# A two-layer graph kernel: waits between engines, the place of TensorE's sums in a sorting stage, and blocks of 2, 4, 4, 6, 6, 6, 4 tiles

## The chip, the core and the metric

The kernel runs on one core of a Trainium2 chip. Its engines work side by side, each through its own queue in order: TensorE (PE, with weight loads shown apart as PEld), VectorE (DVE), ScalarE (ACT), GpSimd (POOL) and SyncE (SP). POOL also issues the indirect DMAs, which fetch or store one row per partition at addresses that are themselves data. The metric is the device time of one execution in microseconds, the median of several.

## The reference, cut to what matters

Two graph layers over 4,096 nodes with 128 features; `adj` has about 64 neighbours for a node.

```
# layer 0: attention with 8 heads
Wh  = einsum('nd,hde->hne', nodes, W)
e   = leaky_relu(f1[:, :, None] + f2[:, None, :])       # f1, f2: Wh times a1, a2
att = softmax(where(adj > 0, e, -9e15))
h   = elu(einsum('hnm,hmd->hnd', att, Wh))
x   = elu(concat(h) @ W1 + b1)
x1  = layernorm(nodes + x, gamma, beta)
# layer 1: quartiles of the kept neighbours, feature by feature
rank = cumsum(mask, axis=1) - 1
skip = where(num_nbr > 5, ceil(num_nbr / 2), 1)
keep = mask & ~(mask & ((rank + 1) % skip == 0))
svals = sort(where(keep, x1, big), axis=1)
agg  = mean over q in (.25, .5, .75) of svals[max(ceil(q * n_keep) - 1, 0)]
agg  = 0.5 * agg + 0.5 * x1
out  = agg @ W.T + b + x1
```

## The kernel before

A tile is 128 nodes, one per partition; there are 32 tiles. The kernel has two stages, `gat` for layer 0 and `sparse` for layer 1. Both gather: a node's neighbours are rows in memory, and each indirect DMA of POOL fetches one neighbour for each of 128 nodes.

**Neighbours (`Front`, within `gat`).** `scan` loads quarters of rows of `adj` (SP, L378, 512 KB each, three buffers), turns them into bits on ACT (L380, L387) and packs them into words by matmuls (L389) in two banks of PSUM. `first` and `second` (L402 on) pull the neighbours' numbers out of the words on DVE, eight at a time with MAX8 and MATCH_REPLACE8 (L188, L190). This goes by blocks of tiles, `BLOCKS = (4, 4, 6, 6, 6, 6)`. When a block's tiles are through, `place` (L447) orders its nodes by their number of neighbours, so that tiles of like counts arise, and POOL scatters the block's lists to `rows_d` (L541, one DMA a tile). From there SP reads each block's lists back (`indices`: ids L903, single columns `others` L919, and info L932). `keep` works out which neighbours layer 1 keeps and writes them to `meta_d` through SP. At the end `order` ranks all nodes by the number they keep, and 32 scatters of POOL write the ranks to `order_d` (L680). `pieces` makes a list of all these steps; `advance(n)` takes the next n of them. The attention's loop calls `advance(2)` once for each half tile, so the search for neighbours of later blocks is laid between the attention of earlier ones. Every engine takes the instructions in the order in which they are written.

**Attention (`gat`).** The loop runs over 64 half tiles. `load` has POOL gather the half tile's neighbours (nb, L971) into a ring of 6 buffers of 18 rows, three half tiles ahead, and once per tile the nodes' own rows (me, L947). `probabilities` computes the softmax (DVE L1054 to L1088, ACT L1073), `rows_sum` spreads the probabilities (DVE L1103) and sums the neighbours by matmuls (PE L1111). After every four half tiles `combine` makes x1 of two tiles, spread over the following half tiles as stages, and two scatters (L1197) write it to `x1_d`. These scatters wait for each other, since all write to the same tensor. After the last gather is issued, the rest of the list is worked off and the 32 scatters to `order_d` are issued:

```
            if u + 3 < 2 * NT:
                held[u + 3] = load(u + 3)
            elif late:
                advance(len(todo))
                for piece in late:
                    piece()
```

**Sorting (`sparse`).** It loads `order` from `order_d`, then for each tile an index row (info, L1867), the nodes' own rows (xs) and 50 to 100 kept neighbours (rows, L1713), again one indirect DMA each. A sorting network runs over a tile's rows, 128 features at once. A step of it is a `compare`: ACT copies the lower rows out (L1751), DVE writes min (L1756) and max (L1757) back. A copy of up to `SMALL = 4` pairs goes to SBUF (low_s), a larger one to PSUM (low, two buffers of four banks with 16 pairs each, so all eight banks). Steps where only one side is needed do without ACT (L1759, L1761). The steps of one tile's last part and the next tile's first part are interleaved. Tile 0's first part is cut into steps of at most `PAIRS // 2` pairs, so that it can begin before all rows have landed.

After a tile is sorted, `quantile` marks the places of the quartiles, and `pick` appends three pieces of work to a list `waiting`: ACT scales the rows at those places (picked, L1810), PE sums them (L1815, L1818) into PSUM, ACT copies the sum to comT (L1823). After four tiles `finish` appends the linear layer on PE (L1835 to L1837), ACT's copy to o (L1841) and the scatters to the output (L1845). Each compare with a copy takes at most one piece from this list. A piece that needs PSUM is taken by a compare of 5 to 12 pairs, and uses the last 512 columns of that compare's own buffer, which the compare leaves free:

```
                if waiting and waiting[0][0] == "copy":
                    waiting.pop(0)[1]()
                elif waiting and SMALL < k <= PAIRS - FOUR:
                    waiting.pop(0)[1](t[:, (PAIRS - FOUR) * D :])
                nc.vector.tensor_tensor(lows, packed, highs, op=ALU.min)
                nc.vector.tensor_tensor(highs, packed, highs, op=ALU.max)
```

The matmuls come before min and max in program order, and since both read or write the same buffer, min waits for the matmuls. What is left in `waiting` after the last tile is done in one go.

Of the kernel before, what the change touches and what calls it, by code (L numbers as in the profile page):

```python
# [50 lines left out]
P = 128  # L51
N = 4096
# [40 lines left out]
MOST = 16  # L93
# [4 lines left out]
BLOCKS = (4, 4, 6, 6, 6, 6)  # L98
# [13 lines left out]
BOUNDS = {  # L112
    4: (
# [203 lines left out]

class Front:
# [88 lines left out]
    def second(self, t, m, k1, cand):  # L407

        nc, one = self.nc, self.one
        k1, cand = k1[:, :m], cand[:, :m]  # L410
        sp = self.spill[:, t : t + m, :]
        wf, base = decode(nc, one, k1, f"1_{m}")
        rest = one.tile([P, m, C1], F32, name=f"rest1_{m}")
        peel(nc, one, wf, base, cand[:, :, :C1], rest, f"1_{m}")
# [5 lines left out]
        k2 = one.tile([P, m, C2], F32, name=f"k2_{m}")  # L420
# [5 lines left out]
        wf, base = decode(nc, one, k2, f"2_{m}")  # L426
        rest = one.tile([P, m, C2], F32, name=f"rest2_{m}")
        peel(nc, one, wf, base, cand[:, :, C1 : C1 + C2], rest, f"2_{m}")
        nc.vector.tensor_scalar(base, base, 127.0 * NG1, None, op0=ALU.add)
        nc.vector.scalar_tensor_tensor(rest, rest, float(NG1), base, op0=ALU.mult, op1=ALU.add)  # L430
        k3 = one.tile([P, m, C3], F32, name=f"k3_{m}")
# [5 lines left out]
        wf, base = decode(nc, one, k3, f"3_{m}")  # L437
        for r in range(PEELS):
            nxt = one.tile([P, m, C3], F32, name=f"rest3_{m}", bufs=2)
            at = C1 + C2 + C3 * r  # L440
            peel(nc, one, wf, base, cand[:, :, at : at + C3], nxt, f"3_{m}")
            wf = nxt
        left = one.tile([P, m], F32, name=f"left_{m}")
# [353 lines left out]
def gat(tc, nc, c, x, adj, xf_d, meta_d, order_d, flag_d, w, a1, a2, w1, b1, gamma, beta, x1_d):  # L797
# [25 lines left out]
    with ExitStack() as ctx:  # L823
# [307 lines left out]
        def combine(t, zT):  # L1131
# [64 lines left out]
            for j in range(TWO):  # L1196
                nc.gpsimd.indirect_dma_start(  # L1197
# [4 lines left out]
                )  # L1202

        held = {u: load(u) for u in range(3)}
# [5 lines left out]
        for u in range(2 * NT):  # L1210
            t, half = divmod(u, 2)
            if u + 3 < 2 * NT:
                held[u + 3] = load(u + 3)
            elif late:

                advance(len(todo))
                for piece in late:
                    piece()
                late = []
# [3 lines left out]
            if u + 1 < 2 * NT:  # L1223
                with ExitStack() as order:
                    for ins in behind:
                        order.enter_context(tc.issue_after(ins))
                    e, behind = probabilities(u + 1, held[u + 1], f1s[(u + 1) // 2])
            with ExitStack() as order:
                for ins in behind:
                    order.enter_context(tc.issue_after(ins))  # L1230
# [7 lines left out]
            advance(2)  # L1238
        for stages in going:
            for _ in stages:  # L1240
                pass
        advance(len(todo))
# [415 lines left out]
def plan(t):  # L1658
# [8 lines left out]
    first = steps(layers[:-merge], lambda i: i, PAIRS if t else PAIRS // 2)  # L1667
# [7 lines left out]
def sparse(tc, nc, c, x1_d, meta_d, order_d, w, b, out):  # L1675


    with tc.tile_pool(name="sp1", bufs=1) as one, tc.tile_pool(
# [15 lines left out]
        it = one.tile([P, 2 * MIDDLE], I32, name="it_p")  # L1694
        nc.gpsimd.iota(it, pattern=[[1, 2 * MIDDLE]], base=0, channel_multiplier=0)
        iota_p = one.tile([P, 2 * MIDDLE], F32, name="iota_p")
        nc.vector.tensor_copy(iota_p, it)
        order = one.tile([P, NT], I32, name="order")
        for i in range(4):
            nc.sync.dma_start(  # L1700
                out=order[:, ts(i, NT // 4)],
                in_=order_d[ts(i, N // 4), :].rearrange("(t p) c -> p (t c)", p=P),
            )

# [7 lines left out]
        def gather(row, info, col):  # L1712
            nc.gpsimd.indirect_dma_start(  # L1713
# [24 lines left out]
        def compare(rows, step):  # L1738
# [4 lines left out]
            if low and high:  # L1743
# [7 lines left out]
                nc.scalar.copy(packed, lows)  # L1751
                if waiting and waiting[0][0] == "copy":
                    waiting.pop(0)[1]()
                elif waiting and SMALL < k <= PAIRS - FOUR:
                    waiting.pop(0)[1](t[:, (PAIRS - FOUR) * D :])
                nc.vector.tensor_tensor(lows, packed, highs, op=ALU.min)  # L1756
                nc.vector.tensor_tensor(highs, packed, highs, op=ALU.max)  # L1757
# [45 lines left out]
        def pick(found, x1, comT):  # L1803
# [3 lines left out]
            def scale():  # L1807
                made["v"] = tp.tile([P, MOST, D], F32, name="picked", bufs=1)
                for i, (v, weight) in enumerate(found):
                    nc.scalar.mul(made["v"][:, i, :], v, weight)  # L1810
# [496 lines left out]
```

## Time and profile before

| | |
|---|---|
| timed runs (3) | 8,432.01 us median, 8,431.48 to 8,434.64 |
| the profiled execution | 7,646.96 us, its span 7,645.2 us |
| first neighbour gather issued | 142.51 us |
| last neighbour gather ends | 3,106.6 us |
| first sorting gather | 3,170.57 us |
| last DVE step ends | 7,632.9 us |
| DVE busy, share of the span | 5,831.7 us, 76% |
| POOL busy, share of the span | 4,343.5 us, 57% |
| ACT busy, share of the span | 2,214.1 us, 29% |
| PE busy, share of the span | 1,122.8 us, 15% |

The profiled execution is 785 us shorter than the timed median. All lines of the profile, and all durations, belong to the profiled one. In the lines, an entry such as `rows<-low,rows` names output and inputs, `x1022` the number of instructions; in the timeline the first two numbers are the start and the duration in us, and the bracket gives the engine's idle time before the instruction and what released it.

### The profile page before, as it was taken

The page shows a single profiled execution, that of the slowest core. Times are in us where ns is not written, and L with a number is a line of the kernel's source. Part 1 is how long each engine was busy: PE and PEld are TensorE (multiplying, and loading weights), DVE is VectorE, ACT ScalarE, POOL GpSimd, SP SyncE. Part 2 cuts the span into 40 slices and gives each one's busy share as a digit, 9 for nine tenths or more (in the row PEclk, how much of TensorE's full clock was granted, in tenths as well). Part 3 has the DMA queues.
Part 4 walks back from the last instruction along what each step waited for, and adds up shares of the span by engine and source line. Part 5 has one row for each costly group of instructions (what it writes and reads, how often), then busy time and mean ns, then how long its engine had stood idle before and what let it go on. Part 6 is the DMA issues. An engine that isn't in the chain of part 4 may idle for free. (4 is left out here: it accounts for less than half of the span.)

```text
span 7645.2 us, 31290 instructions
## 1 busy us (share of the span) xinstructions
PE 1122.8 (15%) x6047; PEld 946.8 (12%) x6047; DVE 5831.7 (76%) x9380; ACT 2214.1 (29%) x2301; POOL 4343.5 (57%) x4524
## 2 busy tenths in 40 slices
PE   3243333322222322100000000000000000000001
PEld 1232222222222222100000000000000000000000
DVE  8465555565223222399999999999999999999999
ACT  6020212100000000144344343434334433443433
POOL 2777677777777777565554645455536434554500
PEclk5566666666566666655555555555555555555555
DMA  6242324222222222111111111111101101111100
GB/s 205 57 121 56 107 62 121 60 55 56 47 56 56 56 56 56 40 44 34 40 35 30 41 31 37 30 36 34 38 23 41 34 24 33 36 35 29 33 1 1
DMA packets 219057, 380.95 MB, mean 50 GB/s; under 512 B 129283, under 2 KB 129412, under 8 KB 218852
## 3 DMA queue, kind: packets, MB, share of 16 engines
q0 software_dynamic: 145808, 308.58, 15.3%
q1 hardware_dynamic: 72898, 70.23, 3.1%
q14 instruction: 156, 1.28, 0.1%
q8 instruction: 49, 0.80, 0.0%
q10 hardware_dynamic: 146, 0.07, 0.0%
HBM read 368.26 MB, written 10.31 MB: 50 GB/s over the span
## 5 line engine op out<-in xcount | busy, mean ns | idle before, releaser
L1713 POOL DMA_INDIRECT rows<-x_d,info x2078 | 2018.2, 971 | 1949.5 <-ACT picked L1810 1270.8
L971 POOL DMA_INDIRECT nb<-xf_d,ids x2190 | 2086.0, 953 | 707.0 <-issue 632.2
L1751 ACT COPY low<-rows 128x2048 f32<-128x2048 f32 (+8 forms) x1022 | 1561.5, 1533 | 2429.9 <-DVE rows L1757 1780.7
L1756 DVE TENSOR_TENSOR rows<-low,rows 128x2048 f32<-128x2048 f32 (+9 forms) x1022 | 1884.7, 1862 | 138.9 <-ACT low L1751 50.0
L1757 DVE TENSOR_TENSOR rows<-low,rows 128x2048 f32<-128x2048 f32 (+9 forms) x1022 | 1882.4, 1861 | 5.8
L1054 DVE TENSOR_TENSOR e<-nb,ps_small 128x64 f32<-128x64 f32 (+9 forms) x200 | 47.7, 240 | 1252.6 <-DMA nb<-xf_d,ids 1206.7
L1111 PE MATMUL ps_z<-spread,nb 128*128 128x128 f32 x4500 | 615.7, 305 | 797.9 <-DVE spread L1103 775.6
L1111 PEld LDWEIGHTS ps_z<-spread,nb 128*128 128x128 f32 x4500 | 604.5, 220 | 829.9 <-DVE spread L1103 420.7
L1815 PE MATMUL low<-sixth_i,picked 128*128 128x128 f32 x300 | 79.8, 442 | 4224.7 <-ACT low L1751 3736.4
L1815 PEld LDWEIGHTS low<-sixth_i,picked 128*128 128x128 f32 x300 | 66.8, 324 | 4237.7 <-ACT low L1751 3744.8
L1073 ACT ACTIVATE ps_e<-e 128x256 f32<-128x256 f32 (+4 forms) x64 | 26.1, 408 | 1936.2 <-DVE e L1054 972.6
L1103 DVE TENSOR_TENSOR spread<-e,ps_small 128x1152 f32<-128x1152 f32 (+4 forms) x312 | 342.7, 1107 | 129.2 <-PE ps_z L1111 79.4
L1845 POOL DMA_INDIRECT out<-o,info x32 | 34.4, 1076 | 392.9 <-ACT o L1841 369.2
L380 ACT ACTIVATE nz<-a_i 128x1024 bf16<-128x1024 int32 x128 | 134.3, 1051 | 292.5 <-DMA a_i<-in_adj 254.3
L1751 ACT COPY low_s<-rows 128x512 f32<-128x512 f32 (+3 forms) x325 | 139.8, 471 | 130.5 <-DVE rows L1756 48.0
L389 PE MATMUL ps_words<-nz,pows 128*128 128x512 bf16 (+1 forms) x272 | 113.7, 577 | 364.4 <-ACT nz L387 258.0
L188 DVE MAX8 k<-key 128x8 f32<-128x256 f32 x416 | 164.6, 412 | 0.7
L1756 DVE TENSOR_TENSOR rows<-low_s,rows 128x512 f32<-128x512 f32 (+3 forms) x325 | 158.3, 500 | 3.0 <-ACT low_s L1751 2.1
L1757 DVE TENSOR_TENSOR rows<-low_s,rows 128x512 f32<-128x512 f32 (+3 forms) x325 | 158.7, 500 | 0.3
L190 DVE MATCH_REPLACE8 key<-k,key 128x256 f32<-128x256 f32 x384 | 155.5, 407 | 0.0
L1142 PE MATMUL ps_h<-zT,w_ga 128*128 128x256 f32 x256 | 116.3, 619 | 198.4 <-DVE s L1414 106.6
L1759 DVE TENSOR_TENSOR rows<-rows 128x256 f32<-128x256 f32 (+8 forms) x245 | 141.6, 580 | 0.2
(246 smaller groups left out, 2528.0 us busy)
## 6 DMA issues: line engine op xcount, KB each, us to landing
a_i<-in_adj SPq DMA_DIRECT2D x128, 512.0 KB
nb<-xf_d,ids POOLq DMA_INDIRECT x2190, 2.5
rows<-x_d,info POOLq DMA_INDIRECT x2078, 2.5
xf_d<-xf POOLq DMA_DIRECT2D x4, 576.0 KB, 7.4
xf<-in_x POOLq DMA_DIRECT2D x4, 512.0 KB
meta_d<-rowdata_k SPq DMA_DIRECT2D x4, 324.0 KB
abc_ta<-in_L_gnn_a POOLq DMA_DIRECT2D x2, 512.0 KB, 7.7
w_ga<-in_L_gnn_W POOLq DMA_DIRECT2D x2, 512.0 KB
```

The costliest lines, as they stand in the source:

```text
L188: nc.vector.max(out=top, in_=work)
L190: nc.vector.match_replace(out=work, in_to_replace=top, in_values=work, imm_value=gone)
L380: nc.scalar.activation(nz[:, j, :], a_i, AF.Relu, scale=-1.0, accum_out=self.negative[:, k : k + 1],)
L971: gather = nc.gpsimd.indirect_dma_start(out=rows[:, used + i, :], out_offset=None, in_=xf_d, in_offset=bass.IndirectOffsetOnAxis(ap=ids[:, ...
L1103: last = nc.vector.tensor_tensor(spread[:, :m], e[:, at : at + m, :].unsqueeze(2).to_broadcast(shape), own.unsqueeze(1).unsqueeze(3).to_br ...
L1111: product = nc.tensor.matmul(ps_z[:, g, :], rows[:, k, :D], spread[:, i].rearrange("p j h -> p (j h)"), start=i0 + i == 0, stop=i0 + i == ...
L1713: nc.gpsimd.indirect_dma_start(out=row, out_offset=None, in_=x1_d, in_offset=bass.IndirectOffsetOnAxis(ap=info[:, col : col + 1], axis=0),)
L1751: nc.scalar.copy(packed, lows)
L1756: nc.vector.tensor_tensor(lows, packed, highs, op=ALU.min)
L1757: nc.vector.tensor_tensor(highs, packed, highs, op=ALU.max)
L1759: nc.vector.tensor_tensor(lows, lows, highs, op=ALU.min)
L1815: nc.tensor.matmul(made["ps"], made["v"][:, i, :], sixth, start=i == 0, stop=False)
```

## The change

- The blocks are `(2, 4, 4, 6, 6, 6, 4)`, with bounds for a block of two. While the half tiles of the first ten tiles run, three steps of the list are taken for each half tile, then two as before.
- The scatters to `x1_d` are declared independent of each other.
- The 32 scatters to `order_d` are placed behind the last gather.
- The rank table (iota_p) is made at the start of the kernel. The loads of `order` and of tile 0's and tile 1's info move from `sparse` into `gat`, ahead of the stages of the last `combine`.
- In `compare`, min and max are declared independent of the matmuls in the other columns of the buffer.
- `pick` puts 22 empty pieces (`APART`) between the scaling and the sums; at most 14 rows (`MOST`) are kept scaled at a time instead of 16.
- Tile 0's first part is cut into steps of at most `PAIRS // 4` pairs.
- `Batches` gives `second` buffers of one size for all batches, where each batch size had its own.

```diff
-MOST = 16
+MOST = 14
+
+APART = 22
...
-BLOCKS = (4, 4, 6, 6, 6, 6)
+BLOCKS = (2, 4, 4, 6, 6, 6, 4)
...
 BOUNDS = {
+    2: (54, 58, 58, 60, 62, 62, 64, 66, 66, 68, 70, 70, 72, 76, 78, 100),
...
+class Batches:
+    def __init__(self, pool):
+        self.pool = pool
+
+    def tile(self, shape, dtype, name, **kw):
+        full = [shape[0], BATCH, *shape[2:]]
+        return self.pool.tile(full, dtype, name=name, **kw)[:, : shape[1]]
...
             for j in range(TWO):
-                nc.gpsimd.indirect_dma_start(
+                done = nc.gpsimd.indirect_dma_start(
                     out=x1_d,
...
+                for other in stored:
+                    tc.declare_no_dep(done.ins, other, reason="each node has a row of its own")
+                stored.append(done.ins)
...
                 advance(len(todo))
-                for piece in late:
-                    piece()
+                with tc.issue_after(gathers[2 * NT - 1][HALF - 1, 0]):
+                    for piece in late:
+                        piece()
...
-            advance(2)
-        for stages in going:
+            advance(3 if u < 2 * START[3] else 2)
+        for stages in going[:-1]:
             for _ in stages:
                 pass
-        advance(len(todo))
+
+        for i in range(4):
+            nc.sync.dma_start(
+                out=order[:, ts(i, NT // 4)],
+                in_=order_d[ts(i, N // 4), :].rearrange("(t p) c -> p (t c)", p=P),
+            )
+        for t, info in enumerate(infos):
+            nc.gpsimd.indirect_dma_start(
+                out=info,
+                out_offset=None,
+                in_=meta_d,
+                in_offset=bass.IndirectOffsetOnAxis(ap=order[:, t : t + 1], axis=0),
+            )
+        for stages in going[-1:]:
+            for _ in stages:
+                pass
...
-    first = steps(layers[:-merge], lambda i: i, PAIRS if t else PAIRS // 2)
+    first = steps(layers[:-merge], lambda i: i, PAIRS if t else PAIRS // 4)
...
+                aside = []
                 if waiting and waiting[0][0] == "copy":
                     waiting.pop(0)[1]()
                 elif waiting and SMALL < k <= PAIRS - FOUR:
-                    waiting.pop(0)[1](t[:, (PAIRS - FOUR) * D :])
-                nc.vector.tensor_tensor(lows, packed, highs, op=ALU.min)
-                nc.vector.tensor_tensor(highs, packed, highs, op=ALU.max)
+                    aside = waiting.pop(0)[1](t[:, (PAIRS - FOUR) * D :])
+                for to, op in ((lows, ALU.min), (highs, ALU.max)):
+                    done = nc.vector.tensor_tensor(to, packed, highs, op=op)
+                    for product in aside:
+                        tc.declare_no_dep(done.ins, product, reason="other columns of the bank")
...
             return [
                 ("copy", scale),
+                *[("copy", lambda: None)] * APART,
                 ("bank", sums),
                 ("copy", lambda: nc.scalar.copy(comT, made["ps"])),
             ]
...
-            info = three.tile([P, MW], I32, name="info", bufs=3 * FOUR)
+            if t < len(infos):
+                info = infos[t]
+            else:
+                info = three.tile([P, MW], I32, name="info", bufs=3 * FOUR)
...
-        gat(tc, nc, c, x, adj, xf_d, meta_d, order_d, flag_d, w, a1, a2, w1, b1, gamma, beta, x1_d)
+        order = keep.tile([P, NT], I32, name="order")
+        infos = [keep.tile([P, MW], I32, name=f"info_{t}") for t in range(2)]
+        it = keep.tile([P, 2 * MIDDLE], I32, name="it_p")
+        nc.gpsimd.iota(it, pattern=[[1, 2 * MIDDLE]], base=0, channel_multiplier=0)
+        iota_p = keep.tile([P, 2 * MIDDLE], F32, name="iota_p")
+        nc.vector.tensor_copy(iota_p, it)
```

`sums` and `layer` return their matmuls, which `compare` needs as `aside`; their sums are the same as before.

## The prediction

> **What bounds the kernel now.** I read the 40 slices of the page first, then its groups, then tables by stage, then the waits of the bounding engine, then single stretches.
>
> ```profile
> DVE  8465555565223222399999999999999999999999
> POOL 2777677777777777565554645455536434554500
> L971 POOL DMA_INDIRECT nb<-xf_d,ids x2190 | 2086.0, 953 | 707.0 <-issue 632.2
> L1756 DVE TENSOR_TENSOR rows<-low,rows 128x2048 f32<-128x2048 f32 (+9 forms) x1022 | 1884.7, 1862 | 138.9 <-ACT low L1751 50.0
> ```
>
> POOL stands at 7 up to slice 16, DVE at 9 from slice 18 on: two stages with different limits. Two stretches of the table by stage (columns: length, then busy time and count of PE, PEld, DVE, ACT, POOL, then TensorE clock, DMA share, GB/s):
>
> ```profile
> 2000.00:2100.00 100.00, 31.68 (x202) 29.25 (x202) 32.83 (x90) 6.39 (x13) 75.62 (x81) 0.62 0.27 56
> 4000.00:5000.00 1000.00, 35.32 (x126) 28.78 (x126) 971.51 (x708) 397.80 (x318) 516.21 (x532) 0.50 0.12 35
> ```
>
> In the attention stage POOL issues 81 indirect DMAs in 100 us: 0.94 us each and 0.30 us up to the next, 1.249 us of POOL's queue, with no gap beyond that. DVE is busy a third. In the sorting stage DVE is busy 97%, POOL half. So in the first stage I count POOL's DMAs and its stalls, in the second DVE's work and its stalls. Where POOL begins and where the stage ends:
>
> ```profile
> 137.15 0.96 POOL L541 DMA_INDIRECT rows_d<-rowdata,pos_i  x1 [0.31 <-issue]
> 142.51 0.99 POOL L971 DMA_INDIRECT nb<-xf_d,ids  x1 [4.40 <-DMA ids<-rows_d]
> ...
> 3105.62 0.94 POOL L971 DMA_INDIRECT nb<-xf_d,ids  x1 [0.30 <-issue]
> 3146.65 0.98 POOL L1197 DMA_INDIRECT x_d<-s,info  x1 [40.09 <-DVE s L1194]
> ...
> 3170.57 0.94 POOL L1713 DMA_INDIRECT rows<-x_d,info  x1 [0.30 <-issue]
> ```
>
> First to last gather takes 2,964 us. In it stand 2,190 nb, 32 me, 28 of 32 rows_d, 32 order_d and 28 of 32 x_d: 2,310 x 1.249 = 2,885, and 79 us remain: 61 in stalls of a microsecond or more between the DMAs, the rest in slightly longer issues. The waits of POOL in this stretch name the large ones:
>
> ```profile
> POOL nb L971 <- PE ps_z L1111: 36.9, 8, 21.6
> POOL me L947 <- DMA info<-rows_d: 12.3, 3, 4.2
> POOL x_d L1197 <- DMA x_d<-s,info: 10.6, 6, 3.2
> ```
>
> (sum, times, longest). For the sorting stage, the waits of DVE from 3,240 us on:
>
> ```profile
> DVE rows L1756 <- ACT low L1751: 46.5, 48, 1.9
> DVE rows L1756 <- PE low L1837: 20.3, 8, 3.3
> DVE rows L1756 <- PE low L1818: 12.3, 10, 2.2
> ...
> 4232.35 1.09 DVE L1756 TENSOR_TENSOR rows<-low,rows 128x896 f32<-128x896 f32 x1 [2.90 <-PE low L1837]
> ```
>
> The last line, from the timeline, is a min that waits for twelve matmuls that the queue put into its bank's tile ahead of it.
>
> **What the Trainium skill says.** "DMA: Bandwidth & Descriptors", "Anatomy of one DMA — SWDGE (gpsimd) path", gives about 2.0 us fixed per DMA up to its semaphore. The trace agrees: an x_d scatter that waits for its predecessor issues 1.52 us after the 0.97 of that one's issue, 2.5 in all. "PSUM — Partial Sum Buffer", "Engine vs sequencer instructions": "ScalarE/VectorE/GpSimdE queues are strict FIFO." The trace agrees: one gather that waited 21.6 us held all behind it. "VectorE: DVE Perf Modes", on the errata for SBUF sources, gives (N+151)/0.96 ns for an fp32 tensor_tensor; the trace has 0.69 for N=512 and 0.96 for 768 (formula 0.96), so a compare cut in two pays some 0.15 us more.
>
> **The change part by part,** against the profiled execution (span 7,645.2 us, 7,646.96 with what lies around it). The median of the timed runs is 8,432, 785 more. No view shows where those lie, so I carry the gain over in absolute time. Were it the POOL queue, a DMA would cost 0.34 more and the part below on its length 8 us more.
>
> *Start: -43.* Block 0 has two tiles instead of four. DVE's drain of two tiles (two x 9 us at `first`, 6 less in `second`, 14 less in the last drains, 7 us of waiting for the tiles' words) goes. The pad memset still holds DVE to 70.6 us, and the ACT copies in `place` stand behind the 27 scan activations queued before them, to about 87. So positions come at about 92 instead of 132.8, two scatters instead of four follow, then 4.4 us for the ids: first nb at 99 instead of 142.5. Bounds 94 to 112, -48 to -30.
>
> *Length of the queue: -30.* Counted in the order of the changed program: nb 2,196, since the bounds of the blocks differ (+6), me 32, rows_d 30, x_d 28, and no order_d: all 32 now stand behind the last gather. 2,286 against 2,310, 24 x 1.249 = 30.
>
> *Stalls in the queue: -24.* Certain in after: about 10 us ahead of me of tile 2, because rows_d of block 1 stand just before it and ids, eight `others` and info follow one another on SP; three times 4.5 at me of tiles 6, 10, 16 behind x_d and info (12.3 for three in before); 14 for what I can't see. 37 against 61. What goes is mostly the 30.1 at 811 and 861. These come from one event: a_i loads on SP stood behind an ids load that waited for POOL, so ACT waited for a_i until 793, its part of e for the next half tile stood behind that, and DVE, PE and the buffers of nb followed. In after SP's ids stand at other places; the worst delay I find is a scan 26 us late in block 3, which has 19 us between `place` and the need by my hand walk of the queues (the other blocks: about 50, 38, 43, 32). Neither end is excluded: -45 if all but the certain ones goes, +40 if that 30 us event comes back and half of it once more.
>
> *End of the attention stage: -5.5.* Behind the last gather POOL has waited 40.1 us for DVE. The 32 order_d (32 x 1.25 = 40) fill that wait, nothing of it is left over by more than a microsecond; then order's load and two infos stand before the last four x_d. Against that the scatters no longer wait for one another (1.52 and 2.55 go), and iota and five infos go from the path to the first sorting gather: 58.5 us after the last gather instead of 64. Bounds 0 to -10; if `s` is there first, order_d is what is late.
>
> *Tile 0 in smaller pieces: -10.7.* The first compare takes six pairs, so twelve gathers, 15.0 us from 3,170.57 to ACT's copy. At four pairs it takes eight, 10. From 3,187 to 3,240 DVE idles 29.7 us. Price: 37 large mins and maxes less, 74 small more, +5 us. Walking the steps with landings 1.25 us apart: -7.5 at the first, -8 of the idle, +5. Bounds 0 to -25.
>
> *Compares no longer wait for matmuls in other columns of their tile: -22.* 32.6 us in the two lines above, some 6 more mixed with ACT. They don't all go: the next-but-one copy on ACT into that tile and its copies of `o` and comT still wait for PE, as at 4,235.54, where ACT stood 8.28 us. About 17 comes back as DVE waiting for ACT. Bounds 0 to -37.
>
> *TensorE's sums 22 compares later (APART): +7.* Within a tile of some 40 compares this costs nothing: the work only stands later in the list. At the end it does. Tile 31's half has too few compares, so tile 30's sums and the layer are issued after the last compare; several `out` scatters, 2.8 us apart, follow instead of one. Before, the end is 8.4 us behind the last DVE step (7,632.9 to 7,641.3); I take 15.5. Bounds 0 to +14.
>
> MOST 14 and the shared tiles (`Batches`) change memory alone. Three list pieces per half tile instead of two until half tile 20 cost no time by themselves: of DVE's 58% from 143 to 1,000 us, the front has about 25 (33% is left without it), so it goes to some 70%.
>
> Sum: -43-30-24-5.5-10.7-22+7 = -128. Profiled 7,519; median 8,304, rounded to **8,303**.
>
> **Rivals.**
> - *The front crowds (20%).* For: DVE at 70% and SP's queue full of a_i early. Against: 43 and 30 are counted, not hoped for. The stalls grow by 36 instead of shrinking by 24: 8,303 + 60 = 8,363.
> - *The sorting stage gives nothing (8%).* For: ACT's 8.28 us wait for the same tile. Against: ACT is busy 40% there (398 of 1,000 us) and has room to catch up. The -22 and -10.7 go: 8,336.
> - *All stalls go (8%).* For: the margins above. Stalls 45 less, sorting 37, tile 0 25: 8,303-21-15-14 = 8,253, or lower with dearer DMAs in the timed runs.
> - *Slower: POOL starves at each edge of a block (7%).* One mechanism: with two and four tiles a block lasts little (141 gathers, 176 us, for the first), its successor's ids come late each time, and all gathers behind it stand, as at 811 and 861, where it cost 30.1 us. Six edges at 30: 8,303 + 181 = 8,484. It decides from 21.5 us per edge. Against: the margins I find are 19 to 50 us at five of six.
> - *No effect (2%).* The scheduler keeps the waits, and the start is eaten later: 8,432.
>
> **How the numbers follow.** 55% for 8,303, whose own bounds give 8,255 to 8,350. Below stands the 8% case, above the crowding and the empty sorting stage; 8 in 10 lie between 8,230 and 8,385. The measurement can tell about 0.2% (17 us) from no change. Faster: 55+20+8+8, less 1 for tails: 0.90; same 0.03; slower 0.07.
>
> **What would show it.** The first nb at about 99 us; 2,286 DMAs in a stretch of about 2,910 from first to last nb; POOL's waits for PE at L1111's successor under 10 us; order_d between the last nb and x_d; the first sorting gather 58 us behind the last nb; DVE's waits for L1818 and L1837 gone, and those for ACT grown by less than 20; the end about 15 us behind DVE's last step. Wrong would be a wait of POOL for PE or info above 60 us in all, or a first nb after 115.

## The result: 8,398 us, and a profile that came from another kind of chip

The changed kernel takes 8,398.3 us (median of six, 8,389.8 to 8,405.5), the kernel before 8,432.3 us beside it. The ratio is 0.996, with a 95% interval of 0.9947 to 0.9973: faster by 34 us, where 129 were forecast (8,432 to 8,303).

One thing has to be known before any other number is read. The runs of this study fell on several chips, and these are of two kinds. On most of them the kernel before takes 8,381 to 8,432 us; on two it takes 7,646 and 7,647. The profile of before that the prediction was made from (7,647 us) is by its length and its waits an execution of the second kind, the timed runs of both kernels are of the first. I call them kind 1 (8,400) and kind 2 (7,650). Most of what follows is about what differs between them. Two simple causes don't fit. The clock granted to TensorE in the profiled executions is 0.545 to 0.548 on kind 1 and 0.551 to 0.554 on kind 2, 1% apart where the times are 10% apart. And a packet of POOL's DMAs takes 144 ns on average in the changed kernel on both kinds (in the kernel before 140 and 129).

The page of the changed kernel, taken on kind 1 (slices, then two groups):

```profile
DVE  5555456446122222224799999999999999999899
POOL 4455554566666666666455456445554645354410
L1783 DVE TENSOR_TENSOR rows<-low,rows 128x2048 f32<-128x2048 f32 (+10 forms) x1970 | 3649.1, 1893 | 88.6 <-ACT low L1776 62.4
L987 POOL DMA_INDIRECT nb<-xf_d,ids x2196 | 2081.9, 948 | 1343.8 <-issue 630.6
```

POOL stands at 4 and 5 in the first slices and never above 6 in the attention stage, where the first profile had 7 nearly throughout. Idle time before its gathers is 1,344 us instead of 707. The waits of POOL between the first and the last gather say for what (sum, times, longest):

```profile
POOL nb L987 <- issue: 630.6, 2063, 1.6
POOL nb L987 <- PE ps_z L1127: 454.9, 25, 49.0
POOL nb L987 <- remote: 223.9, 44, 9.9
```

The first line is the 0.30 us behind each issue. The second is what grew: 36.9 us in the profile before. "Remote" are waits whose end the trace shows only as an update of a semaphore (the counter on which one engine waits for another), with no instruction that ended shortly before. Here the semaphore is PE's in all 44, so these are late results of PE too. Such lines stand in the traces of kind 1 alone. The start and the end of the stage:

```profile
103.23 0.98 POOL L987 DMA_INDIRECT nb<-xf_d,ids  x1 [6.38 <-DMA ids<-rows_d]
...
3789.45 0.96 POOL L694 DMA_INDIRECT order_d<-node,pos_g  x1 [0.30 <-issue]
3796.36 0.98 POOL L1270 DMA_INDIRECT info<-meta_d,order  x1 [5.96 <-DMA order<-order_d]
...
3824.08 0.99 POOL L1213 DMA_INDIRECT x_d<-s,info  x1 [25.47 <-DVE s L1210]
...
3837.67 0.96 POOL L1738 DMA_INDIRECT rows<-x_d,info  x1 [0.30 <-issue]
```

The last gather issues at 3,749.0. The scatters and the two infos stand in the wait for DVE's `s`, as foreseen, and yet `s` comes 75 us behind the last gather, not 40. In the sorting stage no wait of DVE names PE any more (from 3,900 us on):

```profile
DVE rows L1783 <- ACT low L1776: 62.4, 31, 22.5
DVE rows L1783 <- remote: 41.1, 18, 3.2
```

To see what of this comes from the change, the kernel before has to be looked at on the same kind of chip, which is the first experiment.

### The profile page after: what moved, and what is told of

Read it like the earlier page. It is cut to its first block, busy times and chain, and to the rows that moved or that the text cites. A ratio compares the mean times of both kernels' runs of the same rounds, so it can differ in the third digit from the quotient of the medians.

```text
span 8393.7 us, 31590 instructions
## 1 busy us (share of the span) xinstructions
PE 1242.2 (15%) x6061; PEld 1037.3 (12%) x6061; DVE 5891.5 (70%) x9558; ACT 2218.8 (26%) x2340; POOL 4359.9 (52%) x4530
## 5 line engine op out<-in xcount | busy, mean ns | idle before, releaser
L1783 DVE TENSOR_TENSOR rows<-low,rows 128x2048 f32<-128x2048 f32 (+10 forms) x1970 | 3649.1, 1893 | 88.6 <-ACT low L1776 62.4
L1776 ACT COPY low<-rows 128x2048 f32<-128x2048 f32 (+8 forms) x985 | 1528.4, 1557 | 2331.6 <-DVE rows L1783 1695.5
L1127 PE MATMUL ps_z<-spread,nb 128*128 128x128 f32 x4512 | 759.6, 325 | 1345.9 <-issue 747.5
L1119 DVE TENSOR_TENSOR spread<-e,ps_small 128x640 f32<-128x640 f32 (+4 forms) x314 | 343.0, 1106 | 790.2 <-remote 637.7
L1127 PEld LDWEIGHTS ps_z<-spread,nb 128*128 128x128 f32 x4512 | 703.2, 237 | 1424.8 <-issue 961.0
L1783 DVE TENSOR_TENSOR rows<-low_s,rows 128x512 f32<-128x512 f32 (+3 forms) x798 | 395.2, 523 | 127.8 <-remote 40.7
L1776 ACT COPY low_s<-rows 128x512 f32<-128x512 f32 (+3 forms) x399 | 179.9, 486 | 282.8 <-DVE rows L1783 181.8
L1142 ACT COPY zT<-ps_z 128x512 f32<-128x512 f32 x64 | 37.6, 587 | 739.2 <-remote 594.4
L191 DVE MAX8 lists<-cand 128x8 f32<-128x176 f32 x416 | 127.1, 330 | 54.3 <-remote 32.3
L1070 DVE TENSOR_TENSOR e<-nb,ps_small 128x56 f32<-128x56 f32 (+9 forms) x202 | 45.2, 237 | 169.2 <-DMA nb<-xf_d,ids 165.6
```

The source lines that it names most:

```text
L191: nc.vector.max(out=top, in_=work)
L1119: last = nc.vector.tensor_tensor(spread[:, :m], e[:, at : at + m, :].unsqueeze(2).to_broadcast(shape), own.unsqueeze(1).unsqueeze(3).to_br ...
L1127: product = nc.tensor.matmul(ps_z[:, g, :], rows[:, k, :D], spread[:, i].rearrange("p j h -> p (j h)"), start=i0 + i == 0, stop=i0 + i == ...
L1783: done = nc.vector.tensor_tensor(to, packed, highs, op=op)
```

## The experiments

**The kernel before, on kind 1.** No edit.

> The kernel before, unchanged. Its profiled execution shown so far has a span of 7,645 us, its timed runs 8,432. Theory A (the shown execution was an odd one; the kernel usually waits much more in the attention stage): span about 8,430, the attention stage up to the last neighbour gather some 750 us longer than 3,107, POOL waiting for PE or DVE between gathers, and the sorting stage as before, about 4,470 us. Theory B (everything is some 10% slower in the timed runs, the sorting stage too): attention about 3,270 us from first to last gather, sorting about 4,930. Theory C (the profile is what is fast): span near 7,650 again beside a timed 8,430.

Its span is 8,380.7 us, median 8,386.1. None of the theories fits as it stands. A is right that the shown execution was the odd one and that POOL waits much more in the attention stage, but its last gather comes some 535 us later, not 750, and the sorting stage isn't as before. POOL's waits from the first to the last gather:

```profile
POOL nb L971 <- issue: 643.5, 2106, 1.7
POOL nb L971 <- PE ps_z L1111: 398.9, 33, 38.4
POOL nb L971 <- remote: 164.7, 34, 10.0
```

So the kernel before waits as the changed one does. The stretch from first to last gather is 3,497.6 us instead of 2,963.1, and the stage from the first sorting gather (here and below that of tile 0's own rows, xs) to the last compare 4,663.5 instead of 4,463.6. In a steady part without any search, from 3,250 to 3,500 us, POOL gets 176 issues in (in the table by stretch: length, then PE, PEld, DVE, ACT, POOL, TensorE clock, DMA share, GB/s):

```profile
3250.00:3500.00 250.00, 70.90 (x329) 59.54 (x329) 52.70 (x128) 12.70 (x24) 165.84 (x176) 0.58 0.21 49
```

where the full rate, 1.249 us each, would be 200. And in the sorting stage the waits of DVE have become (3,850 to 8,350 us):

```profile
DVE rows L1756 <- remote: 128.0, 5, 42.0
DVE rows L1756 <- issue: 79.9, 23, 32.3
DVE rows L1756 <- ACT low L1751: 36.8, 33, 2.1
```

The two lines on top aren't in the first profile. A single one of these waits, in the timeline:

```profile
4806.22 0.80 PE L1837 MATMUL low<-lwT,comT 128*128 128x128 f32 x2
...
4846.15 1.09 DVE L1756 TENSOR_TENSOR rows<-low,rows 128x896 f32<-128x896 f32 x1 [42.00 <-remote]
```

PE's last matmul of the linear layer is recorded as ended at 4,807.0, and the min that waits for it starts at 4,846.2, 39 us later. In the first profile the same pair stands 0.04 us apart. The trace has the last updates of the semaphore that this min waits for at 4,841.9, 4,844.0, 4,846.1 and 4,846.1: it is PE's release that is recorded late. There are seven such waits in the stage, of 21.4, 42.0, 26.8, 16.4, 32.3, 21.5 and 24.2 us: 185 us, most of the 200 that the stage is longer.

**The two halves of the change, on one chip of kind 1.** First the changed kernel itself.

> The changed kernel, unchanged, on the chip of the next three. All theories: 0 to 50 us below before. Theory A (two parts against each other): its stage from first to last neighbour gather some 100 to 150 us longer than in the kernel before, its sorting stage about 120 us shorter. Theory C (the two traces so far came from two chips, and the stages hardly differ): each stage within 40 us of before.

8,369.8 against 8,386.6 us, ratio 0.9975 [0.9964, 0.9986]. First to last gather 3,626.5 us, so 129 longer than in the trace of the kernel before on kind 1; first sorting gather to last compare 4,538.5, so 125 shorter. Theory A.

The sorting part alone, in the kernel before:

```diff
-MOST = 16
+MOST = 14
+APART = 22
-    first = steps(layers[:-merge], lambda i: i, PAIRS if t else PAIRS // 2)
+    first = steps(layers[:-merge], lambda i: i, PAIRS if t else PAIRS // 4)
... (compare, pick and finish as in the change)
```

> The kernel before with the sorting stage's part of the change alone: min and max not bound to the matmuls in the other columns, sums 22 compares later, tile 0 in smaller pieces. Theory A: 100 to 130 us faster than before, because the seven waits of DVE for the linear layer, 16 to 42 us each in the trace of before on the chip, go. My prediction's sum for these parts: 26 us faster. Theory C: 0 to 40 us faster.

8,266.9 us, ratio 0.9861 [0.9845, 0.9878]: 120 us faster, where the prediction's sum had 26. That is in theory A's range, but not for its reason alone: two of the seven long waits stay, and another edit of this part costs (see below).

The attention part alone, in the changed kernel with `compare`, `pick`, `finish` and tile 0's pieces as before:

> The changed kernel with the sorting stage's compare, pick, finish and tile 0 as before; so the blocks, the scatters and the end of the attention stage alone. Theory A: 70 to 120 us slower than before. My prediction's sum for these parts: 102 us faster. Theory C: within 30 us of before.

8,493.7 us, ratio 1.0123 [1.0106, 1.0140]: 107 us slower, where the prediction's sum had 102 faster. And without the new blocks:

```diff
-BLOCKS = (2, 4, 4, 6, 6, 6, 4)
+BLOCKS = (4, 4, 6, 6, 6, 6)
-            advance(3 if u < 2 * START[3] else 2)
+            advance(2)
```

> The changed kernel with the blocks of before (4, 4, 6, 6, 6, 6) and two list steps for each half tile throughout. Theory A with the blocks as the cause of the longer attention stage: 80 to 140 us faster than before, with the attention stage from first to last gather as long as before or some us shorter, and the first gather back at 143 us. Theory B (the moved order_d scatters, the independent x_d scatters or the moved loads lengthen it): no faster than the changed kernel, attention still 100 us longer than before.

8,251.3 us, ratio 0.9835 [0.9818, 0.9851]. The stretch is 3,470.8 us, 156 shorter than with the new blocks. So the change has two large effects of opposite sign: the sorting part brings 120, the blocks with their pace take 119 back, and the rest is small.

**Which part of the new blocks costs.** Two list steps throughout with the new blocks, and three with the old ones:

```diff
 # first run, in the changed kernel
-            advance(3 if u < 2 * START[3] else 2)
+            advance(2)
 # second run, in the run without the new blocks
-            advance(2)
+            advance(3 if u < 2 * START[3] else 2)
```

> The changed kernel with two list steps for each half tile throughout, its blocks (2, 4, 4, 6, 6, 6, 4) kept. Theory A1 (three steps at a time put too much of the search between two half tiles): 80 us or more faster than the changed kernel, so 100 us faster than before. Theory A2 (the small blocks themselves, each edge with its wait for lists, info and own rows): within 40 us of the changed kernel.

> The run without the new blocks (4, 4, 6, 6, 6, 6), with three list steps for each of the first 28 half tiles. Theory A1: some 80 to 100 us slower than that run's 8,251, so about 40 us faster than before. Theory A2: within 25 us of 8,251.

8,287.7 us, ratio 0.9893 [0.9872, 0.9913], and 8,389.8 us, ratio 1.0009 [1.0000, 1.0017]. So the first gains less against the changed kernel (0.9975) than the 80 us that A1 expected, and the second loses more. The stretch goes from 3,626.5 to 3,537.5 us in the first and from 3,470.8 to 3,595.8 in the second. It is mostly the pace (A1): 89 us with the new blocks, 125 with the old ones, where the faster pace lasts for 28 half tiles instead of 20. The small blocks cost the rest, some 67 us of stretch at two steps (3,537.5 against 3,470.8) and 31 at three, and at two steps their first gather 42 us earlier doesn't pay that back. The trace of the changed kernel from the pair of halves above shows how. In the table by stretch from 844 to 880 us:

```profile
844.00:880.00 36.00, 5.40 (x13) 3.12 (x14) 36.00 (x171) 0.00 (x0) 0.00 (x0) 0.50 0.00 0
```

and in the timeline just before and after it:

```profile
839.75 0.23 DVE L1005 TENSOR_TENSOR mine<-me,group 128x64 f32<-128x64 f32 x1 [16.17 <-DMA me<-xf_d,info]
...
889.11 0.94 POOL L987 DMA_INDIRECT nb<-xf_d,ids  x1 [47.23 <-PE ps_z L1127]
```

First DVE stands 16 us, because one small operation waits for the own rows of the next block's first tile, which POOL can fetch only when that block's lists are back. Then it works 36 us without a pause, and all but one operation of it is search: last drains and `place`, three list steps at once. ACT and POOL do nothing, PE almost nothing. Only at 882.9 comes the next spread (L1119), PE takes it, and POOL's buffer is free at 889. With two steps at a time the longest of POOL's waits for PE is 37.2 us instead of 47.2 with the new blocks, and 36.9 instead of 57.9 with the old ones. Spreading the search further yet, in the run without the new blocks:

```diff
-            advance(2)
+            advance(2 if u < 13 or u % 2 else 1)
```

> The run with two and one list steps by turns again. On a chip with 8,386 before: theory A1 expects 20 to 60 us faster than the 8,251 of the run with two steps throughout, the rival within 15 us of it or slower. On a chip with 7,646: 7,526 again.

8,263.8 against 8,424.9 us, ratio 0.9809 [0.9782, 0.9837]. The run with two steps throughout had 0.9835 [0.9818, 0.9851] on its chip; the intervals overlap, and the stretch, 3,473.7 us, isn't shorter than its 3,470.8. The expected 20 to 60 us are not shown. Both are clearly faster than the changed kernel.

**The order_d scatters.** In the run without the new blocks, the 32 scatters where they were:

```diff
-                with tc.issue_after(gathers[2 * NT - 1][HALF - 1, 0]):
-                    for piece in late:
-                        piece()
+                for piece in late:
+                    piece()
```

> The run without the new blocks, with the 32 order_d scatters issued in the loop as before. Theory D (beside POOL's scatters PE and DVE go slower, so the last sums come late and the 40 us of scatters in the wait for them are not free): 10 to 25 us faster than 8,251; first sorting gather 50 to 60 us behind the last neighbour gather instead of 86. Rival (the scatters fill idle time of POOL): 15 to 25 us slower than 8,251, because 32 issues come back into the stretch.

8,259.3 us, ratio 0.9856 [0.9839, 0.9872], against 0.9835: not told apart, and the gain of 10 to 25 us that theory D expected is not shown. What happens is seen, though. The stretch gets 25 us longer, and the first sorting gather comes 53.8 us behind the last gather instead of 86.2. So the move that looked free gains 25 and loses 32. Where it loses, in the run without the new blocks (scatters at work from 3,615 to 3,655 us), PE and then DVE:

```profile
3650.67 0.37 PE L1127 MATMUL ps_z<-spread,nb 128*128 128x128 f32 x1 [2.53 <-issue]
3653.47 0.37 PE L1127 MATMUL ps_z<-spread,nb 128*128 128x128 f32 x1 [2.43 <-issue]
3656.27 0.37 PE L1127 MATMUL ps_z<-spread,nb 128*128 128x128 f32 x1 [2.43 <-issue]
...
3666.14 2.42 DVE L1119 TENSOR_TENSOR spread<-e,ps_small 128x640 f32<-128x640 f32 x3 [30.02 <-remote]
```

and the same place in the run with the sorting part alone, where POOL has nothing to do there:

```profile
3653.30 9.76 PE L1113 MATMUL ps_z<-spread,nb 128*128 128x128 f32 x86
...
3654.17 0.82 DVE L1105 TENSOR_TENSOR spread<-e,ps_small 128x640 f32<-128x640 f32 x1 [4.93 <-PE ps_z L1113]
```

86 matmuls in 9.8 us with POOL quiet; with POOL scattering single ones 2.8 us apart at the end of its burst, and a wait of 30.0 us instead of 4.9. That is the mechanism to test.

**POOL quiet in the sorting stage.**

```diff
-            for s in range(HIGH[t]):
+            for s in range(HIGH[t] if t < 3 else 0):
 # (rows of tiles 0 to 2 are kept and sorted again; their unused part is set to zero)
```

> The kernel before, whose sorting stage gathers neighbours for tiles 0 to 2 alone and sorts these rows again for the other tiles: it leaves out 29 tiles' gathers, some 1,900 DMAs, so the output differs from there on. Theory D (waits for PE end late where POOL issues DMAs beside it): DVE's waits for the linear layer, 16 to 42 us each on the chip, fall to about 3 us as in the first profile; last DVE step about 4,480 us after the first sorting gather instead of 4,675. Rival (PE is late by itself after a pause): they stay at 16 us or more, and the stage within 60 us of 4,675.

The waits of DVE in that stage, over the same window:

```profile
DVE rows L1756 <- ACT low L1751: 44.2, 44, 1.9
DVE rows L1756 <- PE low L1837: 20.3, 8, 3.3
DVE rows L1756 <- PE low L1818: 12.3, 10, 2.2
```

These are, number for number in the two PE lines, the waits of the first profile, on a chip of kind 1. From the first sorting gather to the last compare it takes 4,480.6 us. So on kind 1 PE's results come late where POOL's DMAs run beside it, and not where they don't. The run leaves out the transfers together with their issues, so it doesn't say which of the two does it.

**The two edits of the sorting stage apart.** Freed min and max without the empty pieces, and the empty pieces with min and max bound (both with tile 0's smaller pieces):

```diff
 # first
-APART = 22
+APART = 0
 # second
-                    aside = waiting.pop(0)[1](t[:, (PAIRS - FOUR) * D :])
+                    waiting.pop(0)[1](t[:, (PAIRS - FOUR) * D :])
```

> The sorting part alone without the 22 empty pieces again. On a chip with 8,386 before: theory S1 8,255 to 8,285, theory S2 8,305 to 8,350. On a chip with 7,646: 7,599 again.

> The sorting part alone with the 22 empty pieces, min and max bound to the matmuls, a last time. On the first kind of chip theory S3 (the two edits only work together) expects it within 30 us of before, with seven waits of DVE for PE of 16 to 42 us; theory S4 (the distance alone brings the gain) 80 to 120 us faster. On the second kind: 13 us faster again.

8,445.1 us, ratio 1.0028 [1.0016, 1.0040], and 8,317.3 us, ratio 0.9921 [0.9904, 0.9938]: 20 us slower than before and 70 us faster. Both lie outside what their theories expected. Freeing min and max leaves the seven long waits as they were: each moves one engine on. Without the empty pieces, ACT and then DVE:

```profile
4949.88 0.58 ACT L1858 COPY o<-low 128x512 f32<-128x512 f32 x1 [44.71 <-remote]
...
4952.19 4.22 DVE L1760 TENSOR_TENSOR rows<-low,rows 128x1792 f32<-128x1792 f32 x2 [42.23 <-issue]
```

ACT's copy of `o` waits for PE, the compares' copies stand behind it, and DVE waits for those: 42.2 us, where the kernel before had 42.0. The empty pieces take most of these waits away, and they do so because they move PE's work in time. POOL gathers the next tile in a burst at the start of each tile and then waits for a free buffer; 22 compares later it is mostly through. Counted from the traces, for each linear layer of the first seven groups: POOL's DMAs from 10 us before to 10 us after its first matmul, and DVE's longest gap from there on up to 60 us behind the last.

```
                                    DMAs : gap in us
kernel before              16:21.4  16:42.0  15:26.8  13:16.4  16:32.3  16:21.5  16:24.2
freed, no empty pieces     16:21.5  16:42.2  16:24.9  14:17.8  16:34.5  16:22.7  16:19.6
empty pieces, bound        12: 2.1  14: 3.0   6: 2.9   3: 2.9   9: 1.5  16:16.3  16:21.3
both                        3: 3.0   7: 2.7   3: 1.7   3: 0.3   8: 0.5  14:13.7  15:22.5
```

In 18 of the 28 the gap is 13.7 to 42.2 us, with 13 to 16 DMAs; in nine, with 12 or fewer, it is 3.0 at most. One doesn't fit a count alone: 14 DMAs and 3.0 us. There the burst has only just begun, with 6 DMAs in the 20 us before the first matmul, where the 18 late ones have 10 to 16. Tiles with many neighbours still have the burst running 22 compares later, so the last two gaps stay in every version. A larger distance for these was not tried.

That isn't the whole of these two runs, since both have tile 0's smaller pieces. In the first 200 us of the sorting stage there are no sums yet (PE does nothing), so the pieces are all that differs there. The kernel before and the empty pieces alone, first on kind 2, then on kind 1 (third, DVE's busy time):

```profile
3171.00:3371.00 200.00, 0.00 (x0) 0.00 (x0) 151.23 (x144) 65.15 (x68) 151.94 (x158) 0.50 0.19 52
3170.00:3370.00 200.00, 0.00 (x0) 0.00 (x0) 159.62 (x219) 71.70 (x105) 152.76 (x156) 0.50 0.20 51
...
3706.00:3906.00 200.00, 0.00 (x0) 0.00 (x0) 139.09 (x131) 60.02 (x63) 151.58 (x159) 0.50 0.21 52
3709.00:3909.00 200.00, 0.00 (x0) 0.00 (x0) 87.89 (x154) 41.89 (x79) 154.01 (x151) 0.50 0.20 49
```

On kind 2 the pieces let DVE do 8 us more work, on kind 1 51 us less: its 154 operations there are 0.61 us long on average (131 of 1.1 us before), and it idles 112 of the 200 us. Until DVE has done its first 250 us of work in the stage it has idled 68.4 us in the kernel before on kind 1 and 125 to 129 in every trace with the smaller pieces there; on kind 2 it is 52.4 and 41 to 42. So on kind 1 the pieces cost some 59 us, on kind 2 they bring 11. From there on DVE idles 276 us in the kernel before on kind 1, 236 with min and max freed, 134 with the empty pieces, 89 with both. Freeing does bring 40 us, then, out of shorter waits than the seven, and the smaller pieces hide it; the distance brings 142. No run has the other edits of the sorting stage with tile 0's pieces as before.

**The same kernels on kind 2.** Some runs fell on chips of the second kind, where the prediction's profile came from.

> The changed kernel a last time, for the second kind of chip. There theory D expects 7,500 to 7,560, its rival 7,600 to 7,650. On the first kind: 0.996 of before again.

The changed kernel takes 7,554.0 against 7,647.4 us there, ratio 0.9877 [0.9861, 0.9894]: 93 us faster. POOL's waits from its first to its last gather:

```profile
POOL nb L987 <- issue: 648.5, 2128, 0.3
POOL nb L987 <- PE ps_z L1127: 79.9, 8, 47.2
POOL me L963 <- DMA info<-rows_d: 23.5, 4, 11.1
```

On the other chip of kind 2, the run with two and one steps by turns takes 7,526.2 against 7,645.9 us, ratio 0.9842 [0.9826, 0.9859]. What was expected of this run and of the two after it is given in times of kind 1, so it can't be held against them.

> The run without the new blocks, with two list steps for each of the first 13 half tiles, then two and one by turns. Theory A1 (what the search does between two half tiles delays PE and so POOL): 20 to 60 us faster than the 8,251 of that run, since the search is spread further. Rival (the search costs what it costs, and only its total counts, or a later list is missed): within 15 us of 8,251, or slower.

Freed min and max without the empty pieces take 7,598.9 us, ratio 0.9938 [0.9922, 0.9955], and the empty pieces alone 7,633.2, ratio 0.9983 [0.9976, 0.9989]. Counted as above, past DVE's first 250 us of work, freeing brings 39 us of idle time, as on kind 1, and the distance 11 instead of 142. Here PE is never late, so what counts is that min no longer waits for the matmuls, and their place in time hardly does.

> The run with the sorting part alone, without the 22 empty pieces: sums taken as soon as before. Theory S1 (freeing min and max from the matmuls brings it all): within 15 us of that run's 8,267. Theory S2 (the sums' distance matters too, because ACT's copies of the sums and the next copy into the buffer wait for PE just as late): 40 to 80 us slower than 8,267, with waits of DVE for ACT in place of those for PE.

> The run with the sorting part alone, with the 22 empty pieces, but min and max bound to the matmuls again. Theory S1: the gain of 120 us is gone, 0 to 15 us slower than before, with seven waits of DVE of 16 to 42 us as in the kernel before. Theory S2: 40 to 80 us faster than before.

A further run of the changed kernel on kind 1 (8,391.4 against 8,424.9 us, ratio 0.9959 [0.9949, 0.9969]) and a second one of the empty pieces alone on kind 2 (0.9981 [0.9973, 0.9989]) repeat what is said above.

## Why the prediction was wrong, step by step

The step that failed is the one that the sum was laid on: "No view shows where those lie, so I carry the gain over in absolute time." The 785 us between the profiled execution and the timed runs were not a constant beside the kernel. They lay in the very waits that the change moves: of the 735 between the two spans of the kernel before, 534 from the first to the last gather and 200 in the sorting stage. A second step failed on both kinds, and so in the prediction's own terms: "Stalls in the queue: -24" came out at about +39 on kind 2 (9.2 us longer from first to last gather, with 24 DMAs fewer). The profile of before was, but for one line named below, read rightly for the execution that it shows, and that execution wasn't one of the timed kind. With the profiled spans (before 7,645.2 and 8,380.7 us, changed 7,552.2 and 8,371.2):

| step | predicted | kind 2 | kind 1 |
|---|---|---|---|
| first nb | -43 | -41.5 | -42.6 |
| first to last nb | -54 | +9.2 | +128.9 |
| last nb to first sorting gather | -5.5 | -5.5 | +22.3 |
| first sorting gather to last compare | -32.7 | -61.9 | -125.0 |
| of it tile 0 (DVE's idle time in its first 250 us of work) | -10.7 | -11.0 | +59.3 |
| last compare to the end | +7 | +6.8 | +6.9 |
| sum (without the line on tile 0) | -128 | -92.9 | -9.5 |

- *Start:* right. The first nb issues at 101 to 103 us (predicted 99) on both kinds, behind the ids as before.
- *Length of the queue:* the count of DMAs is right, 2,286 in both traces. On kind 1 a shorter queue is worth less, since POOL gets 176 issues where 200 would fit: it is not the bound there but waits for PE's release of the buffers. The move of order_d alone still took some 25 us out of the stretch.
- *Stalls in the queue:* this term has the wrong sign on both kinds. I took 37 us in after, 14 of them for "what I can't see". Measured on kind 2 are 79.9 for PE and 23.5 for info. The hand walk asked whether each block's lists are there in time, and they mostly are; it never asked how long DVE works on the search between two spreads. One stall of 47.2 us on kind 2 (DVE stands 23.9 us for `me`, then works 41 us without a pause), and its like on kind 1, come from that. The rival "the front crowds" named this mechanism, with DVE's load as its ground; its size, 36 us more than before, is near the 39 of kind 2 (43.0 more for PE, 11.2 for info, less elsewhere); kind 1 has 129 us more in the stretch. The prediction's own sign of being wrong, waits for PE or info above 60 us in all, came: 103.4 on kind 2. With the old blocks and two and one steps by turns the stretch on kind 2 is 2,906.6 us, 56.5 shorter than before.
- *End of the attention stage:* exact on kind 2. On kind 1 "they fill that wait" fails: `s` waits for PE, and beside the scatters PE is late.
- *Tile 0:* right on kind 2, and the first compare comes 7.4 us earlier (predicted 7.5). On kind 1 the same edit costs 59 us, which no view of the first profile could show.
- *Compares and sums:* mis-sized. I had 17 of 39 us come back as waits of DVE for ACT. On kind 2 that doesn't happen: over the like window DVE's waits for ACT's two copies are 31.4 and 1.5 us, against 46.5 and 1.4 before, and without tile 0 the stage is 50.9 us shorter instead of 22. The line named for the 17 us was misread:

```profile
4235.54 1.66 ACT L1751 COPY low<-rows 128x1792 f32<-128x1792 f32 x1 [8.28 <-DVE rows L1757]
```

The 8.28 us are a wait for DVE, not for PE. On kind 1 the seven long waits, 185 us, came to be gained as well.
- *APART:* I gave it a cost at the end and nothing else. The cost is right (+6.8). That it moves PE's work out of POOL's burst, worth some 142 us of DVE's idle time on kind 1, could not be seen in a profile without late waits.
- *The sum:* it gives 8,303.8, so 8,304; 8,303 was put down. The 2.5 us of a DMA up to its semaphore, said to agree with 2.0, are half a us more; no term rests on it.

The Trainium skill's sentence in "PSUM — Partial Sum Buffer", "Engine vs sequencer instructions", that these engines' queues are strict FIFO, was cited for POOL. It bears on DVE's new stalls as well: one small operation that waits for `me` holds 36 us of search and all spreads behind it, and the trace shows just that (16.17 us of wait, then 36.00 of 36 us busy).

The version that beats both kernels on both kinds is the changed one with the old blocks and two and one list steps by turns: 0.981 of before on kind 1, 0.984 on kind 2. With two steps throughout it is 0.984 on kind 1; that was not run on kind 2.

## What to carry to other kernels

When a profiled execution is 10% shorter than the timed ones, find out where the difference lies before any gain is worked out, best by a profile of the same program from a timed run; a gain can't be carried across as a constant if the missing time lies in the waits that the change touches. When background work is laid between pieces of a pipeline, ask for its longest run on the engine that feeds the pipeline, not only for its total and its due times. When a wait is removed, look for the next instruction that needs the same result: freeing min and max shortened none of the seven long waits as long as ACT waited for the same matmuls. And when several edits are timed together, look at the stretch where only one of them acts: the total of the sorting part, 120 us faster, hid an edit that cost 59.

## What the runs showed of the hardware

On kind 1 PE's semaphore was updated up to 39 us after PE's recorded end in the kernel before, and 43 in the run of the attention part alone, where a burst of POOL's indirect DMAs had run for a while and still went on. Where the burst was over, or left out, the update came in time; on kind 2 DVE's waits for PE in the sorting stage are 3.3 us at most. The counts behind this were made for the linear layers of the sorting stage. Beside such bursts on kind 1 single matmuls stand 2.8 us apart (0.37 us each), and short MAX8 operations of DVE likewise: in the kernel before, at 162.7 and 165.5 us, 0.43 us each. Long operations keep their duration: the 128x2048 min is 2.28 us on both kinds. That fits the cost of tile 0's pieces, which are short. The Trainium skill says in "Perfetto Trace Analysis", "Tensor Engine Instruction (MATMUL, LD_WEIGHTS)", that PE's end in a profile is estimated and its semaphore follows later; on kind 2 the estimate is right to 0.04 us for the min above, on kind 1 the waiting engine has to be read instead.

What makes the two kinds differ isn't settled. It may lie in the chip, or in the recording of events: for the same kernel before, the trace of kind 1 holds 24,305 updates of semaphores and that of kind 2 87,013 (of DVE's own 5,652 and 7,981), so many are missing from the record on kind 1. The timed runs contain the delay, and no run here tells the two apart.
